# Moving the first two layernorms and the last sequence's attention and shared-expert sums inside a one-core transformer block

## The chip, the cores and the metric

The kernel runs on one core of a Trainium2 chip. The metric is the device time of one execution in microseconds (us). The unchanged kernel has a median of 1045.91 us over 3 runs (1045.9 to 1046.4). Engines are named as in the profile: PE (matrix multiply, with PEld for its weight loads), DVE (vector), ACT (activation), POOL (the engine that also issues indirect DMAs), SP (the queue that issues most plain DMAs).

## The reference, cut to what matters

The input is 16 sequences of 512 tokens of 256 numbers, float32. Each token gets its input, plus linear attention over its own sequence, plus a feed-forward part:

```python
xn = layernorm(x)
q, k, v = elu(xn@Wq+bq)+1, elu(xn@Wk+bk)+1, xn@Wv+bv          # 16 heads of 16
kv  = einsum('bkhd,bkhm->bhdm', k, v)
att = einsum('bqhd,bhdm->bqhm', q, kv) / max(q . sum(k), 1e-6) @ Wo + bo
shared = swiglu(xn @ w_in.T) @ w_out.T
# two of the four experts of the winning group, weights w_se
routed = sum_e (swiglu(xn @ w1.T) * w_se[:, e]) @ w2[e].T
out = x + att + shared + routed
```

## The kernel before, in words

The work is done in two stages. **The first stage** goes over the 16 sequences (`for b in range(B)`). For sequence b it makes keys, queries and the router's logits (`project`, L404 and L415), the routing decisions (`route`, nearly all small DVE instructions), x'k (`summarize`, `pxk`, L681), the routed experts' hidden rows (`hidden_rows`, `phr`, L587; `first_rows`, L636 for sequence 0), which go to the DRAM tensor `h_d`, and the shared expert's hidden columns (`hidden`, `phs`, L613; `first_hidden`, L655 for sequence 0), which stay in `hs_all`. `mix` (L694 to L717) turns x'k into the matrix `kvo`: four products `pvk` on PE, `vk` on DVE, two products `pm` on PE, a copy on ACT. `outputs` (L750) then sums, for each of the four tiles of 128 tokens, four products with `hs_all` and two with `qT` and `kvo` into `po`; `gather` adds that to the residual `res` (L761) and writes it to the right part of the token's row in `h_d` (L762). The projections of sequence b+1 are put in front of the rest of sequence b, and the layernorm of b+2 beside it.

**The second stage** runs over 67 tiles of 128 tokens, sorted by their pair of experts (`order` computes the sorting as a list of row numbers, in the last two sequences). Tiles are taken in pairs (`Tiles`). `rows` gathers the rows of a pair from `h_d` with one indirect DMA per tile on POOL (L902) into one of four buffers, which are the old arrays `qq_all`, `x_all`, `kk_all`, `xn_all` in turn. `turn` transposes the pair's hidden rows into `hT` (two buffers), with 12 copies on ACT (L923) and seven transposes on DVE (L929, L935). `sums` does the products with the two experts' weights on PE (`py`, L952: 8 records of 512 columns for a tile, in one of six PSUM buffers), adds the weighted products to the tile's residual part on DVE (L959, L962) and scatters the result to `out` with an indirect DMA on POOL (L965). Gathers run three pairs ahead, turns two.

**The last sequence (b = 15) is handled apart.** Its residual, without `po`, goes to `h_d` early (L999), so that it passes through the second stage like any other. Its `mix` stands inside the second stage (after the fourth pair, L1059), and its four `po` at the very end: the first before the `If` that handles surplus tiles (L1063), the other three after it. There the finished output of sequence 15 is read back from DRAM (`far`, L1081), `po` is added (L1088), and the result is written again (L1089).

**The start.** `first` does the layernorm and projections of sequence 0 in an order pinned by hand (`tc.keep_in_program_order`), tile by tile: statistics (L327, L328), root on ACT (L329), reciprocal and scaling on DVE (L330, L331), transpose on PE (L336), copy on ACT (L339), with the key and query products (L343) between the tiles. `normalize(1)` (L285 to L305) does sequence 1 without a pinned order. For later sequences `normalize` sends the result through DRAM and transposes it on DVE (L264).

What sets the order elsewhere: the program is a list of statements that a scheduler turns into one queue for each engine, by its own estimates of cost; `pin`ned statements keep their written order, `issue_after` holds a statement behind another, `high_priority` moves one up. Each engine then works its queue strictly in order.

Of the kernel before, what the change touches and what calls it, by code (L numbers as in the profile page):

```python
# [15 lines left out]
P = 128  # L16
# [5 lines left out]
def block_kernel(  # L22
# [248 lines left out]
    def normalize(b):  # L271

        xt = xs[b]
        st = small.tile([P, NT, 6], FP, tag="st", name=f"st_{b}")
        mv = small.tile([P, NT, 2], FP, tag="mv", name=f"mv_{b}")
        sd = small.tile([P, NT], FP, tag="sd", name=f"sd_{b}")
        rs = small.tile([P, NT], FP, tag="rs", name=f"rs_{b}")
        xn = xn_all[:, b % 2]

        n = 1 if b == 0 else NT  # L280
        made = []
        for g in range(0, NT, n):
            with tc.issue_after(last_xn[-1].ins) if last_xn else nullcontext():
                for t in range(g, g + n):
                    nc.vector.bn_stats(out=st[:, t, :], in_=xt[:, t, :])  # L285
            for t in range(g, g + n):
                nc.vector.bn_aggr(out=mv[:, t, :], in_=st[:, t, :])
            with tc.issue_after(last_copy[-1].ins) if last_copy else nullcontext():
                nc.scalar.activation(sd[:, g : g + n], mv[:, g : g + n, 1], AF.Sqrt, bias=eps_sb)
            nc.vector.reciprocal(rs[:, g : g + n], sd[:, g : g + n])  # L290
            for t in range(g, g + n):
                made.append(nc.vector.tensor_scalar(
                    xn[:, t, :], xt[:, t, :], mv[:, t, 0:1], rs[:, t : t + 1],
                    ALU.subtract, ALU.mult,
                ))
        last_xn[:] = made[-1:]
        xnT = work.tile([P, KD, S], FP, tag="xnT", name=f"xnT_{b}")
        if b < 2:
            for t in range(NT):
                pt = ps_mm.tile([P, KD, P], FP, tag="mm", name=f"pt_{b}_{t}")  # L300
                for c in range(KD):
                    nc.tensor.transpose(
                        pt[:, c, :], xn[:, t, :].rearrange("p (m c) -> p c m", c=KD)[:, c], ident
                    )
                last_copy.append(nc.scalar.copy(xnT[:, :, ts(t, P)], pt))  # L305
            return xn, xnT, None
        last_copy.clear()
        nc.sync.dma_start(out=xn_d[b % 2].rearrange("(t p) d -> p t d", p=P), in_=xn)
        return xn, xnT, turn(xnT, xn_d[b % 2], "xb", b, "(i c)")

    def first():

        pin = tc.keep_in_program_order
        xt, xn, kk, qq = xs[0], xn_all[:, 0], kk_all[:, 0], qq_all[:, 0]
        st = small.tile([P, NT, 6], FP, tag="st", name="st_0")
        mv = small.tile([P, NT, 2], FP, tag="mv", name="mv_0")
        sd = small.tile([P, NT], FP, tag="sd", name="sd_0")  # L320
        rs = small.tile([P, NT], FP, tag="rs", name="rs_0")
        lg = small.tile([P, NT, E + G], FP, tag="lg", name="lg_0")
        xnT = work.tile([P, KD, S], FP, tag="xnT", name="xnT_0")
        pks, pqs = [], []

        def place(t):
            pin(nc.vector.bn_stats(out=st[:, t, :], in_=xt[:, t, :]))  # L327
            pin(nc.vector.bn_aggr(out=mv[:, t, :], in_=st[:, t, :]))  # L328
            pin(nc.scalar.activation(sd[:, t : t + 1], mv[:, t, 1:2], AF.Sqrt, bias=eps_sb))  # L329
            pin(nc.vector.reciprocal(rs[:, t : t + 1], sd[:, t : t + 1]))  # L330
            last_xn[:] = [pin(nc.vector.tensor_scalar(  # L331
                xn[:, t, :], xt[:, t, :], mv[:, t, 0:1], rs[:, t : t + 1], ALU.subtract, ALU.mult
            ))]
            pt = ps_mm.tile([P, KD, P], FP, tag="mm", name=f"pt_0_{t}")
            for c in range(KD):
                pin(nc.tensor.transpose(  # L336
                    pt[:, c, :], xn[:, t, :].rearrange("p (m c) -> p c m", c=KD)[:, c], ident
                ))
            last_copy[:] = [pin(nc.scalar.copy(xnT[:, :, ts(t, P)], pt))]  # L339

        def times(to, t, w):
            for k in range(KD):
                pin(nc.tensor.matmul(  # L343
                    to, lhsT=xnT[:, k, ts(t, P)], rhs=w[:, k, :], start=(k == 0), stop=(k == KD - 1)
                ))
# [9 lines left out]

        place(0)
        place(1)
        keys(0)
        keys(1)
        queries(0)  # L360
        place(2)
        queries(1)
        keys(2)
        place(3)
        keys(3)
        queries(2)
        queries(3)
        for t in range(NT):
# [6 lines left out]
        return xn, xnT, (qq, kk, lg)  # L375

# [8 lines left out]
    def feature_map(b, y, tag):  # L385
# [8 lines left out]
        nc.vector.scalar_tensor_tensor(y, y, 0.0, low, ALU.max, ALU.add)  # L394

# [204 lines left out]

    def hidden(b, xs7):

# [21 lines left out]

        seven(f"phs_{b}", product, split, room, done, lambda n: None)
        return h, made
# [61 lines left out]

    def mix(b, xk, ksb):

        pvk = ps_mm.tile([P, KD, P], FP, tag="mm", name=f"pvk_{b}")
        for c in range(KD):
            for k in range(KD):
                nc.tensor.matmul(  # L694
                    pvk[:, c, :], lhsT=wv_sb[:, k, ts(c, P)],
                    rhs=by_quadrant(xk[:, k, :])[:, c],
                    start=(k == 0), stop=(k == KD - 1),
                )
        vk = one.tile([P, KD, P], FP, tag="vk", name=f"vk_{b}")

        with tc.high_priority():
# [8 lines left out]
            )  # L710
        pm = ps_mm.tile([P, KD, D], FP, tag="mm", name=f"pm_{b}")
        for c in range(KD):
            nc.tensor.matmul(
                pm[:, c, :], lhsT=vk[:, c, :], rhs=wo_sb[:, c, :], start=True, stop=True
            )
        kvo = one.tile([P, KD, D], FP, tag="kvo", name=f"kvo_{b}")
        nc.scalar.copy(kvo, pm)  # L717
        return kvo
# [21 lines left out]
    def outputs(b, t, qT, kvo, hs):  # L740


        if b + 2 < B or (b + 1 == B and t == 0):
            po = ps_y.tile([P, D], FP, tag="py", name=f"po_{b}_{t}")
# [4 lines left out]
        for i, (a, w) in enumerate(parts):  # L749
            step = nc.tensor.matmul(po, lhsT=a, rhs=w, start=(i == 0), stop=(i == len(parts) - 1))  # L750
            if b + 1 == B:
                tc.keep_in_program_order(step)
        return po

    def gather(b, res, qT, kvo, hs, placed, then):

        for t in range(NT):
# [4 lines left out]
            nc.sync.dma_start(out=h_d[ts(b * NT + t, P), HID:ROW], in_=res[:, t, :])  # L762
            between(b, then(t))

    def order():
# [216 lines left out]

    *normed_0, (qq, kk, lg) = first()
    normed = {0: (*normed_0, None), 1: normalize(1)}
    res = residual(0)
    feature_map(0, kk, "km")
    feature_map(0, qq, "qm")
    route(0, lg, res)
# [3 lines left out]
    for b in range(B):  # L992
# [38 lines left out]
        if b + 1 == B:  # L1031
            for w in tiles[:AHEAD]:
                w.rows()
        hs, made = hidden(b, sums7) if b else first_hidden(xnT)
        if b + 1 < B:
            kvo = mix(b, xk, ksb)
        if b + 2 == B:
            next(steps_of_order)
        if b + 1 < B:
            gather(b, res, qT, kvo, hs, normed[b + 2][2]() if b + 2 < B else None, {0: 2, 1: 2, 3: 2}.get)  # L1040
# [7 lines left out]

    for i, w in enumerate(tiles[: AHEAD - 1]):

        w.turn(made[i])
# [21 lines left out]


    first_po = outputs(B - 1, 0, qT, kvo, hs)
    rest(SURE)


    for half, queue in enumerate((nc.sync, nc.scalar)):
        far = work.tile([P, 2, D], FP, tag="hr", name=f"far_{half}", bufs=4)  # L1080
        queue.dma_start(  # L1081
            out=far, in_=out[B - 1, ts(half, 2 * P), :].rearrange("(t p) d -> p t d", p=P)
        )
        for j in range(2):
            t = 2 * half + j
            po = outputs(B - 1, t, qT, kvo, hs) if t else first_po
            y = work.tile([P, D], FP, tag="y", name=f"last_{t}", bufs=4)
            nc.vector.tensor_tensor(y, po, far[:, j], ALU.add)  # L1088
            (nc.sync, nc.scalar)[t % 2].dma_start(out=out[B - 1, ts(t, P), :], in_=y)  # L1089

# [31 lines left out]
```

## Time and profile before

| what | us |
|---|---|
| median of 3 runs | 1045.91 |
| the profiled execution | 1045.97 |
| its span in the profile | 1044.2 |
| time outside the span | 1.77 |
| PE busy | 1011.8 (97% of the span) |
| first matmul of sequence 0 starts | 5.30 |
| keys of sequence 1 start (L404) | 23.14 |
| last `phs` of sequence 15 ends | 784.11 |
| first `py` of the second stage starts | 792.48 |
| first of the last four `po` starts | 1029.41 |
| last PE work ends | 1040.63 |

How to read it: all times are from the start of the span of one profiled execution. A record in the PE rows is one pass of the array; a float32 product of 128x256 appears as two records. A wait is the idle time of an engine just before an instruction, put down to whatever released it.

### The profile page before, as it was taken

Reading aid. Unit: us, or ns where it says so; the run is one execution under the profiler, and the core shown is the slowest. Engines: PE = TensorE matmul, PEld = TensorE weight load, DVE = VectorE, ACT = ScalarE, POOL = GpSimd, SP = SyncE. Lnnn points to the kernel's source line nnn. Section 1 sums busy time; section 2 is a strip of 40 time slices with the busy share of each in tenths; the row PEclk is TensorE's granted clock in tenths of the full one; section 3 lists DMA queues with packets and bytes.
Section 4 is the critical chain, followed back from the end, with each engine's and each line's share of the span. In section 5 each row is a group of like instructions: output and inputs, shape, how many; then the busy total and the mean of one; then the engine's idle time right before and its main releaser. Section 6 shows DMA issues by size and latency. Waiting matters only on the chain. (4 is left out here: it accounts for less than half of the span.)

```text
span 1044.2 us, 12410 instructions
## 1 busy us (share of the span) xinstructions
PE 1011.8 (97%) x3704; PEld 685.2 (66%) x3704; DVE 787.8 (75%) x1976; ACT 479.1 (46%) x886; POOL 242.3 (23%) x353
## 2 busy tenths in 40 slices
PE   6999999999999999999999999999896999999998
PEld 4566868677786868686777768686672444444445
DVE  5969797978788797878786877868975666666662
ACT  2415353534344352535344443425138666667770
POOL 5202020110202021110202020211022555565541
PEclk9999999999999999999999999999998999999999
DMA  7142624425151523314141313221253445544441
GB/s 217 42 138 87 174 87 116 127 71 151 51 161 49 162 78 87 121 42 141 41 121 56 115 57 114 84 61 61 60 141 127 142 137 154 160 149 149 149 125 69
DMA packets 130436, 114.24 MB, mean 109 GB/s; under 512 B 72605, under 2 KB 114589, under 8 KB 130368
## 3 DMA queue, kind: packets, MB, share of 16 engines
q1 hardware_dynamic: 120080, 77.42, 25.3%
q0 software_dynamic: 8912, 35.21, 11.2%
q10 hardware_dynamic: 1376, 0.80, 0.3%
q8 instruction: 31, 0.51, 0.2%
q14 instruction: 37, 0.30, 0.1%
HBM read 63.52 MB, written 50.27 MB: 109 GB/s over the span
## 5 line engine op out<-in xcount | busy, mean ns | idle before, releaser
L952 PE MATMUL py<-w_sb,hT 128*128 x536 | 233.1, 598 | 8.4 <-DMA w_sb<-in_w 8.4
L952 PEld LDWEIGHTS py<-w_sb,hT 128*128 128x128 f32 x536 | 102.7, 192 | 137.7 <-issue 137.7
L750 PE MATMUL po<-wout_sb,hs_all 128*128 128x256 f32 x512 | 124.9, 382 | 1.9 <-DVE hs_all L572 1.4
L382 POOL TENSOR_TENSOR res<-x_all,bo_sb 128x256 f32<-128x256 f32 x64 | 49.0, 796 | 271.7 <-DMA h_d<-res 204.9
L750 PEld LDWEIGHTS po<-wout_sb,hs_all 128*128 128x128 f32 x512 | 95.8, 191 | 17.4 <-DVE hs_all L572 3.4
L965 POOL DMA_INDIRECT out<-y,goal x67 | 67.8, 1012 | 104.3 <-DVE y L962 95.1
L761 DVE TENSOR_TENSOR res<-po,res 128x256 f32<-128x256 f32 x60 | 25.5, 424 | 74.7 <-PE po L750 72.0
L668 POOL TENSOR_TENSOR k<-kk_all 128x512 f32<-128x512 f32 x16 | 20.9, 1309 | 261.8 <-DVE sm L450 251.9
L750 PE MATMUL po<-kvo,qT 128*128 128x256 f32 x256 | 65.9, 383 | 0.0
L587 PE MATMUL phr_w<-w_sb,ss 128*128 128x512 f32 x120 | 62.2, 600 | 3.6 <-DVE hr L566 2.2
L613 PE MATMUL phs_w<-ss,win_sb 128*128 128x256 f32 x240 | 61.6, 379 | 0.0
L613 PE MATMUL phs_t<-xnT,win_sb 128*128 128x256 f32 x240 | 61.6, 379 | 0.0
L587 PE MATMUL phr_t<-w_sb,xnT 128*128 128x512 f32 x120 | 61.3, 593 | 0.0
L404 PE MATMUL pk<-wkr_sb,xnT 128*128 128x266 f32 x240 | 58.9, 395 | 0.3 <-ACT xnT L305 0.3
L613 PE MATMUL phs_t<-ss,win_sb 128*128 128x256 f32 x240 | 59.1, 379 | 0.0
L587 PE MATMUL phr_t<-w_sb,ss 128*128 128x512 f32 x120 | 59.0, 593 | 0.0
L390 ACT ACTIVATE km<-km 128x1024 f32<-128x1024 f32 x16 | 16.9, 1058 | 90.7 <-DVE km L389 90.7
L681 PE MATMUL pxk<-kk_all,xn_all 128*128 128x256 f32 x256 | 57.9, 379 | 0.0
L923 ACT COPY hb<-qq_all 32x256 f32<-32x256 f32 x108 | 43.4, 402 | 26.2 <-DMA qq_all<-h_d,source 22.8
L415 PE MATMUL pq<-w_sb,xnT 128*128 128x256 f32 x240 | 54.2, 379 | 0.0
L750 PEld LDWEIGHTS po<-kvo,qT 128*128 128x128 f32 x256 | 47.5, 190 | 8.9 <-ACT kvo L717 3.0
L681 PEld LDWEIGHTS pxk<-kk_all,xn_all 128*128 128x128 f32 x256 | 48.6, 190 | 6.6
(215 smaller groups left out, 1936.3 us busy)
## 6 DMA issues: line engine op xcount, KB each, us to landing
h_d<-hr SPq DMA_DIRECT2D x64, 256.0 KB, 2.4
q_d<-qq_all SPq DMA_DIRECT2D x16, 512.0 KB, 2.8
qb<-q_d SPq DMA_DIRECT2D x64, 128.0 KB, 3.0
w_sb<-in_w SPq DMA_DIRECT2D x64, 128.0 KB, 3.5
h_d<-res SPq DMA_DIRECT2D x60, 129.0 KB, 1.9
x_all<-in_x SPq DMA_DIRECT2D x15, 512.0 KB, 5.3
xn_d<-xn_all SPq DMA_DIRECT2D x14, 512.0 KB, 3.5
xb<-xn_d SPq DMA_DIRECT2D x56, 128.0 KB, 3.0
```

The costliest lines, as they stand in the source:

```text
L382: nc.gpsimd.tensor_tensor(res[:, t, 0:D], xt[:, t, :], bo_sb, ALU.add)
L404: nc.tensor.matmul(pk, lhsT=xnT[:, k, ts(t, P)], rhs=wkr_sb[:, k, :], start=(k == 0), stop=(k == KD - 1),)
L415: nc.tensor.matmul(pq[:, t, :], lhsT=xnT[:, k, ts(t2 + t, P)], rhs=wq_sb[:, k, :], start=(k == 0), stop=(k == KD - 1),)
L587: tc.keep_in_program_order(nc.tensor.matmul(to, lhsT=xs7[i][:, ts(u, P)], rhs=w1_in[W7[i]], start=start, stop=stop, skip_group_check=True,))
L613: tc.keep_in_program_order(nc.tensor.matmul(split(to)[:, f, :], lhsT=win_in[W7[i]][:, ts(2 * u + f, P)], rhs=xs7[i], start=start and f == ...
L668: nc.gpsimd.tensor_tensor(k2, kk[:, 0:2, :], kk[:, 2:4, :], ALU.add)
L681: nc.tensor.matmul(pxk[:, c, :], lhsT=xn[:, t, ts(c, P)], rhs=kk[:, t, :], start=(t == 0), stop=(t == NT - 1),)
L750: step = nc.tensor.matmul(po, lhsT=a, rhs=w, start=(i == 0), stop=(i == len(parts) - 1))
L761: nc.vector.tensor_tensor(res[:, t, 0:D], po, res[:, t, 0:D], ALU.add)
L923: nc.scalar.copy(there[ts(q, Q), a - near, 0:n, :], self.hg[ts(a, Q), 0:n, ts(q, W)])
L952: nc.tensor.matmul(py.rearrange("p j d -> p (j d)"), lhsT=self.hT[:, f, ts(j, P)], rhs=w2_sb[:, f, bass.ds(regs[i % TR], 2 * D)], start=(f ...
L965: stored = nc.gpsimd.indirect_dma_start(out=out_rows, out_offset=bass.IndirectOffsetOnAxis(ap=self.goal[:, i : i + 1], axis=0), in_=y, in_ ...
```

## The change

Three things are done.

1. **The start.** The layernorm of sequence 1 is moved into `first`, and both are pinned: all four tiles of sequence 0 are measured and scaled, with the transposes one tile behind; then the keys, then the queries; then the bias additions, the statistics of sequence 1 between them; then its scaling and its transposes. The residual of sequence 0 is told to follow the query feature map.
2. **The last sequence.** `mix` is split in `values` (`pvk`, `vk`) and `mix` (`pm`, `kvo`). For sequence 15 both are put inside `hidden`, after the third and the ninth of its fourteen products, in PSUM buffers of the other pool (`py`). After `hidden`, the first two turns are written, and `gather_last` does all 48 records of `po` in two PSUM buffers (first all products with `kvo`, then all with `hs_all`), adds them to `res` and writes it to `h_d` in two DMAs of 256 tokens. The block at the end of the kernel (read back, add, write again) is gone.
3. **The second gather.** The first three pairs are still gathered early, for their hidden rows. Pairs 0 and 1 are gathered again in front of the loop, and pair 2 inside its first round behind the gathers of pair 3, so that their residual part is the finished one.

```diff
     def first():
+        for t in range(NT):
+            measure(0, t)
+            scale(0, t, 1)
+            if t:
+                place(0, t - 1)
+        keys(0)
+        place(0, NT - 1)
+        for t in range(1, NT):
+            keys(t)
+        for t in range(NT):
+            queries(t)
+        for t in range(2):
+            keep(t)
+        for t in range(NT):
+            measure(1, t)
+        for t in range(2, NT):
+            keep(t)
+        scale(1, 0, NT)
+        for t in range(NT):
+            place(1, t)
...
+    with tc.issue_after(feature_map(0, qq, "qm").ins):
+        res = residual(0)
...
+    def gather_last(b, res, qT, kvo, hs):
+        pos = [ps_y.tile([P, 2, D], FP, tag="py", name=f"po_{b}_{i}") for i in range(NT // 2)]
...
+        for t in range(NT):
+            add([(qT[:, c, ts(t, P)], kvo[:, c, :]) for c in range(KD)], t, True, False)
+        for t in range(NT):
+            add([(hs[:, f, ts(t, P)], wout_sb[:, f, :]) for f in range(KH)], t, False, True)
+        for i, po in enumerate(pos):
+            to = res[:, 2 * i : 2 * i + 2, 0:D]
+            with tc.high_priority():
+                nc.vector.tensor_tensor(to, po, to, ALU.add)
+            nc.sync.dma_start(
+                out=h_d[ts(b * NT // 2 + i, 2 * P), HID:ROW].rearrange("(t p) h -> p t h", p=P),
+                in_=res[:, 2 * i : 2 * i + 2, :],
+            )
...
+            def then(n):
+                if n == 2:
+                    made_of["vk"] = values(b, xk, ksb)
+                if n == 8:
+                    made_of["kvo"] = mix(b, made_of["vk"])
...
+        if b + 1 == B:
+            for i, w in enumerate(tiles[: AHEAD - 1]):
+                w.turn(made[i])
+            gather_last(b, res, qT, kvo, hs)
...
+    for w in tiles[: AHEAD - 1]:
+        w.rows()
     for g, w in enumerate(tiles):
         if g + AHEAD < len(tiles):
             tiles[g + AHEAD].rows()
         if g + AHEAD - 1 < len(tiles):
             tiles[g + AHEAD - 1].turn()
+        if g == 0:
+            tiles[AHEAD - 1].rows()
         w.sums()
-        if g == AHEAD:
-            kvo = mix(B - 1, xk, ksb)
...
-    first_po = outputs(B - 1, 0, qT, kvo, hs)
     rest(SURE)
-    for half, queue in enumerate((nc.sync, nc.scalar)):
-        far = work.tile([P, 2, D], FP, tag="hr", name=f"far_{half}", bufs=4)
...
-            po = outputs(B - 1, t, qT, kvo, hs) if t else first_po
-            y = work.tile([P, D], FP, tag="y", name=f"last_{t}", bufs=4)
-            nc.vector.tensor_tensor(y, po, far[:, j], ALU.add)
-            (nc.sync, nc.scalar)[t % 2].dma_start(out=out[B - 1, ts(t, P), :], in_=y)
```

More of the change, by code (lines that the diff above doesn't have):

```diff
@@ L278, in normalize @@
         xn = xn_all[:, b % 2]
-        n = 1 if b == 0 else NT
         made = []
-        for g in range(0, NT, n):
+        for g, n in [(0, NT)]:
             with tc.issue_after(last_xn[-1].ins) if last_xn else nullcontext():
@@ L297, in normalize @@
         xnT = work.tile([P, KD, S], FP, tag="xnT", name=f"xnT_{b}")
[L298 to L306, printed above, removed]
         last_copy.clear()
@@ L316, in first @@
         pin = tc.keep_in_program_order
[L317 to L321, printed above, removed]
+        stats = []
+        for b in range(2):
+            stats.append([
+                small.tile([P, NT, n], FP, tag=tag, name=f"{tag}_{b}")
+                for tag, n in (("st", 6), ("mv", 2), ("sd", 1), ("rs", 1))
+            ])
@@ L322, in first, with measure @@
+        kk, qq = kk_all[:, 0], qq_all[:, 0]
         lg = small.tile([P, NT, E + G], FP, tag="lg", name="lg_0")
-        xnT = work.tile([P, KD, S], FP, tag="xnT", name="xnT_0")
+        xnT = [work.tile([P, KD, S], FP, tag="xnT", name=f"xnT_{b}") for b in range(2)]
         pks, pqs = [], []
-        def place(t):
-            pin(nc.vector.bn_stats(out=st[:, t, :], in_=xt[:, t, :]))
+        def measure(b, t):
+            st, mv, _, _ = stats[b]
+            pin(nc.vector.bn_stats(out=st[:, t, :], in_=xs[b][:, t, :]))
@@ L328, in place, with scale @@
             pin(nc.vector.bn_aggr(out=mv[:, t, :], in_=st[:, t, :]))
[L329 to L334, printed above, removed]
+        def scale(b, t, n):
+            _, mv, sd, rs = stats[b]
+            pin(nc.scalar.activation(sd[:, t : t + n, 0], mv[:, t : t + n, 1], AF.Sqrt, bias=eps_sb))
+            pin(nc.vector.reciprocal(rs[:, t : t + n], sd[:, t : t + n]))
+            for i in range(t, t + n):
+                last_xn[:] = [pin(nc.vector.tensor_scalar(
+                    xn_all[:, b, i, :], xs[b][:, i, :], mv[:, i, 0:1], rs[:, i], ALU.subtract, ALU.mult
+                ))]
@@ L335, in place @@
+        def place(b, t):
+            pt = ps_mm.tile([P, KD, P], FP, tag="mm", name=f"pt_{b}_{t}")
             for c in range(KD):
                 pin(nc.tensor.transpose(
-                    pt[:, c, :], xn[:, t, :].rearrange("p (m c) -> p c m", c=KD)[:, c], ident
+                    pt[:, c, :], xn_all[:, b, t, :].rearrange("p (m c) -> p c m", c=KD)[:, c], ident
                 ))
-            last_copy[:] = [pin(nc.scalar.copy(xnT[:, :, ts(t, P)], pt))]
+            last_copy[:] = [pin(nc.scalar.copy(xnT[b][:, :, ts(t, P)], pt))]
@@ L343, in times @@
                 pin(nc.tensor.matmul(
-                    to, lhsT=xnT[:, k, ts(t, P)], rhs=w[:, k, :], start=(k == 0), stop=(k == KD - 1)
+                    to, lhsT=xnT[0][:, k, ts(t, P)], rhs=w[:, k, :], start=(k == 0), stop=(k == KD - 1)
                 ))
@@ L354, in queries, with keep @@
             times(pqs[-1][:, t % 2, :], t, wq_sb)
[L356 to L368, printed above, removed]
+        def keep(t):
             pin(nc.vector.tensor_tensor(kk[:, t, :], pks[t][:, 0:D], bkr_sb[:, 0:D], ALU.add))
             pin(nc.vector.tensor_tensor(lg[:, t, :], pks[t][:, D:KR], bkr_sb[:, D:KR], ALU.add))
+        for t in range(NT):
[18 more added lines that the diff above has]
+            place(1, t)
         for i, pq in enumerate(pqs):
@@ L374, in first @@
             )
-        return xn, xnT, (qq, kk, lg)
+        return xnT, (qq, kk, lg)
     def residual(b):
@@ L393, in feature_map @@
             nc.scalar.activation(low, low, AF.Exp, scale=-1.0)
-        nc.vector.scalar_tensor_tensor(y, y, 0.0, low, ALU.max, ALU.add)
+        return nc.vector.scalar_tensor_tensor(y, y, 0.0, low, ALU.max, ALU.add)
     def project(b, xnT):
@@ L599, in hidden_rows, with hidden @@
         seven(f"phr_{b}", product, lambda a: a, room, done, lambda n: between(b, then(n)))
-    def hidden(b, xs7):
+    def hidden(b, xs7, then=lambda n: None):
         h = hs_all
@@ L623, in done @@
                 made.append((silu, product))
-        seven(f"phs_{b}", product, split, room, done, lambda n: None)
+        seven(f"phs_{b}", product, split, room, done, then)
         return h, made
@@ L687, in summarize, with small_sums, values @@
         return xk
-    def mix(b, xk, ksb):
-        pvk = ps_mm.tile([P, KD, P], FP, tag="mm", name=f"pvk_{b}")
+    def small_sums(b, shape, name):
+        if b + 1 == B:
+            return ps_y.tile(shape, FP, tag="py", name=f"{name}_{b}"), tc.keep_in_program_order
+        return ps_mm.tile(shape, FP, tag="mm", name=f"{name}_{b}"), lambda step: step
+    def values(b, xk, ksb):
+        pvk, pin = small_sums(b, [P, KD, P], "pvk")
         for c in range(KD):
             for k in range(KD):
-                nc.tensor.matmul(
+                pin(nc.tensor.matmul(
                     pvk[:, c, :], lhsT=wv_sb[:, k, ts(c, P)],
@@ L697, in mix @@
                     start=(k == 0), stop=(k == KD - 1),
-                )
+                ))
         vk = one.tile([P, KD, P], FP, tag="vk", name=f"vk_{b}")
@@ L710, in mix @@
             )
-        pm = ps_mm.tile([P, KD, D], FP, tag="mm", name=f"pm_{b}")
+        return vk
+    def mix(b, vk):
+        pm, pin = small_sums(b, [P, KD, D], "pm")
         for c in range(KD):
-            nc.tensor.matmul(
+            pin(nc.tensor.matmul(
                 pm[:, c, :], lhsT=vk[:, c, :], rhs=wo_sb[:, c, :], start=True, stop=True
-            )
+            ))
         kvo = one.tile([P, KD, D], FP, tag="kvo", name=f"kvo_{b}")
-        nc.scalar.copy(kvo, pm)
+        with tc.high_priority() if b + 1 == B else nullcontext():
+            nc.scalar.copy(kvo, pm)
         return kvo
@@ L740, in outputs @@
     def outputs(b, t, qT, kvo, hs):
-        if b + 2 < B or (b + 1 == B and t == 0):
+        if b + 2 != B:
             po = ps_y.tile([P, D], FP, tag="py", name=f"po_{b}_{t}")
@@ L749, in outputs @@
         for i, (a, w) in enumerate(parts):
-            step = nc.tensor.matmul(po, lhsT=a, rhs=w, start=(i == 0), stop=(i == len(parts) - 1))
-            if b + 1 == B:
-                tc.keep_in_program_order(step)
+            nc.tensor.matmul(po, lhsT=a, rhs=w, start=(i == 0), stop=(i == len(parts) - 1))
         return po
@@ L763, in gather, with add @@
             between(b, then(t))
+    def gather_last(b, res, qT, kvo, hs):
+        pos = [ps_y.tile([P, 2, D], FP, tag="py", name=f"po_{b}_{i}") for i in range(NT // 2)]
+        def add(parts, t, begin, end):
+            for i, (a, w) in enumerate(parts):
+                tc.keep_in_program_order(nc.tensor.matmul(
+                    pos[t // 2][:, t % 2, :], lhsT=a, rhs=w, start=begin and i == 0 and t % 2 == 0,
+                    stop=end and i == len(parts) - 1, skip_group_check=True,
+                ))
+        for t in range(NT):
[10 more added lines that the diff above has]
+            )
     def order():
@@ L981, in block_kernel @@
     waiting = list(range(G * NL))
-    *normed_0, (qq, kk, lg) = first()
-    normed = {0: (*normed_0, None), 1: normalize(1)}
-    res = residual(0)
+    first_xnT, (qq, kk, lg) = first()
+    normed = {b: (xn_all[:, b], first_xnT[b], None) for b in range(2)}
     feature_map(0, kk, "km")
-    feature_map(0, qq, "qm")
+    with tc.issue_after(feature_map(0, qq, "qm").ins):
+        res = residual(0)
     route(0, lg, res)
@@ L1033, in block_kernel @@
                 w.rows()
-        hs, made = hidden(b, sums7) if b else first_hidden(xnT)
         if b + 1 < B:
-            kvo = mix(b, xk, ksb)
+            hs, made = hidden(b, sums7) if b else first_hidden(xnT)
+            kvo = mix(b, values(b, xk, ksb))
+        else:
+            def then(n):
[3 more added lines that the diff above has]
+                    made_of["kvo"] = mix(b, made_of["vk"])
+            made_of = {}
+            hs, made = hidden(b, sums7, then)
+            kvo = made_of["kvo"]
         if b + 2 == B:
             next(steps_of_order)
-        if b + 1 < B:
+        if b + 1 == B:
+            for i, w in enumerate(tiles[: AHEAD - 1]):
+                w.turn(made[i])
+            gather_last(b, res, qT, kvo, hs)
+        else:
             gather(b, res, qT, kvo, hs, normed[b + 2][2]() if b + 2 < B else None, {0: 2, 1: 2, 3: 2}.get)
@@ L1047, in block_kernel @@
     )
-    for i, w in enumerate(tiles[: AHEAD - 1]):
-        w.turn(made[i])
+    for w in tiles[: AHEAD - 1]:
+        w.rows()
     for g, w in enumerate(tiles):
@@ L1072, in rest @@
                 rest(i + STEP)
-    first_po = outputs(B - 1, 0, qT, kvo, hs)
     rest(SURE)
-    for half, queue in enumerate((nc.sync, nc.scalar)):
-        far = work.tile([P, 2, D], FP, tag="hr", name=f"far_{half}", bufs=4)
[L1081 to L1085, printed above, removed]
-            po = outputs(B - 1, t, qT, kvo, hs) if t else first_po
-            y = work.tile([P, D], FP, tag="y", name=f"last_{t}", bufs=4)
-            nc.vector.tensor_tensor(y, po, far[:, j], ALU.add)
-            (nc.sync, nc.scalar)[t % 2].dma_start(out=out[B - 1, ts(t, P), :], in_=y)
 def kernel(**inputs):
```

## The prediction

> **What bounds the kernel now.** I read the busy shares first, then what the tensor engine waits for, then the chain that ended last, and only then the three places that the change touches. Lines of the page:
>
> ```profile
> PE 1011.8 (97%) x3704; PEld 685.2 (66%) x3704; DVE 787.8 (75%) x1976; ACT 479.1 (46%) x886; POOL 242.3 (23%) x353
> ...
> PE 1%; DVE 0%; issue 0%
> ```
>
> PE is busy 97% of the span, so 1044.2 - 1011.8 = 32.4 us is all that can be won without taking work from PE. The chain holds only the last 1%: before it PE simply works on. So the question is where those 32 us lie. The waits of PE (line waited for, by whom: us in total, times, longest):
>
> ```profile
> PE py L952 <- DMA w_sb<-in_w: 8.4, 1, 8.4
> PE pt L336 <- DVE xn_all L331: 7.0, 2, 5.3
> PE pm L713 <- DVE rz L729: 2.5, 1, 2.5
> PE phr_w L587 <- DVE hr L566: 2.2, 7, 0.3
> PE pt L302 <- DVE xn_all L292: 2.2, 1, 2.2
> PE pm L713 <- DVE vk L708: 2.2, 1, 2.2
> ```
>
> Row 1 is the step from the first to the second stage, rows 2 and 5 are the start, row 6 is the late `mix` of the last sequence. Row 4 is nearly all that PE waits between 80 and 730 us, so the sequences in the middle run at PE's pace. The windows show that an idle PE costs twice (window, length, busy PE, PEld, DVE, ACT, POOL, granted clock, DMA share, GB/s):
>
> ```profile
> 23.00:27.00 4.00, 3.85 (x10) 3.04 (x11) 2.48 (x8) 1.30 (x6) 0.20 (x1) 0.57 0.27 97
> ...
> 784.00:792.00 8.00, 0.10 (x1) 0.00 (x0) 6.46 (x15) 7.59 (x18) 0.25 (x1) 0.73 0.89 299
> 792.00:796.00 4.00, 3.52 (x4) 1.50 (x5) 1.58 (x4) 3.85 (x11) 0.00 (x0) 0.50 0.01 4
> 824.00:828.00 4.00, 2.09 (x7) 1.44 (x8) 3.54 (x10) 2.50 (x7) 1.04 (x2) 1.00 0.56 182
> ```
>
> PE stands still from 784.11 to 792.48, and then runs at a clock of .50. After the shorter idle of row 5, at 21.4, it ran at .57; after row 6's 2.2 us, at 826, it kept 1.00.
>
> **Change 1, the start: -3.0.** Before, the root of tile 3 stands on ACT behind the copy of tile 2, which waited for PE:
>
> ```profile
> 13.52 0.37 ACT L339 COPY xnT<-pt 128x256 f32<-128x256 f32 x1 [4.58 <-PE pt L336]
> ...
> 21.40 1.45 PE L302 MATMUL pt<-ident,xn_all 128*128 128x128 f32 x8 [2.22 <-DVE xn_all L292]
> 23.14 5.47 PE L404 MATMUL pk<-wkr_sb,xnT 128*128 128x266 f32 x16 [0.30 <-ACT xnT L305]
> ```
>
> After, no root waits for PE: the first three tiles took 2.4 us each from statistics to scaling (statistics at 5.07, 7.50 and 9.55), so tile 3 is scaled at about 9.9 instead of 15.2. PE then does the first keys to 10.9 (still slow: .47 us a record), the other twelve key records and tile 3's transposes to 14.9, 16 query records of .215 to 18.3. DVE has, behind the keys of 0 and 1 (13.7), the statistics of sequence 1 (2.4, to 16.2), the other bias additions (to 17.3), `qq` (.7) and the four scalings (1.4): 19.6. The transposes end at 20.1, and sequence 1's keys, 16 x .223 = 3.6 us at full clock in place of 5.47, at 23.7 instead of 28.5: a lead of 4.7.
>
> The lead isn't all kept, since DVE becomes late. x_2's load is issued at 19.90 behind the weights, and its statistics waited for it until 24.52; nothing moves that load. The residual told to follow the feature map keeps its place in POOL's order, so this instruction of the diff costs nothing; what hides it is POOL, 23% busy. `pxk` of sequence 0 needs the key feature map, about 27.5: lead 4.4. Then DVE works without a gap to 64 us; of its work only some 1.2 us has been done earlier, and each `phs` L655 (50.49, .37 waited for `hr` L643) needs a buffer that DVE frees: lead 3.1 there. At `pm` L713 (66.95, freed by `vk` L708 at 66.86) it is 2.8 to 3.0, with one `qT` transpose of 1.24 now queued behind `vk`. I take -3.0; the ends are -4.7 (all kept) and 0 (DVE bound by x_2's load all the way). From there PE bounds, and the lead stays. DVE's order in the middle is shuffled by small statements; bounds ±3.3, what PE waits there in all; I take 0.
>
> **Change 2a, between the stages: -2.1.** Before, from the end of `phs` (784.11) to the end of `py` (1029.41), 245.3 us: 8.37 idle, 2.9 lost to the clock (5.4 us at half pace), 67 tiles x 3.43 = 229.7, `pvk` and `pm` 1.7, their wait 2.17, and .46 of small gaps. After: `pvk` and `pm` (1.7) stand inside `hidden`, between products, six of the fourteen products apart, so that PE has other work while DVE makes `vk`; 48 records of `po` x .2145 = 10.3 fill the idle, in which the weights of the second stage land anyway (they let `py` go at 792.48, and `po` ends at 796); so neither the 8.4 nor the 2.9 nor the 2.17 return. 1.7 + 10.3 + 229.7 + .46 + 1.0 (change 3) = 243.2 against 245.3: -2.1, bounds with those of change 3. The `po` work itself, 10.3, is only moved: it is taken off in the tail's sum.
>
> If the cover fails, that is if `po` had to wait for `res` or `kvo`, the price would be the idle again, up to 2.9 of clock besides. Here `kvo` is due five products ahead, and the products with `hs_all` stand last in `po`; so I count none. The skill has a rule on this: the Trainium skill, "TensorE: Matmul & The Clock Gate", Part 1, says that the clock falls only after an idle window of about 3.4 us and needs about 3.4 us of work to come back. The trace differs from it: 2.2 us of idle at 21.4 sufficed for .57, and after 8.4 us the half pace lasted 5.4. By the page the clock's price would be an estimated 1.7 in place of 2.9, and the time 1.2 later than mine.
>
> **Change 3, the second gathers: +1.0 of stalls (counted above), 0 to +5.8.** They are six more indirect DMAs on POOL. One is issued in about 1.0 (the 67 scatters L965: 1012 ns) and landed 3.7 to 3.9 after its issue (8.7 at most, beside weight loads). They wait for both `res` writes: the last `po` (796 on the clock of before), the addition on DVE in the order between the two thirds of `hT_2` (798.3), the write of 264 KB (2.4, as `h_d<-hr`): 800.8. Then POOL issues pairs 0 and 1 (801.0 to 805.8), pair 3's two, and the first scatters; queued behind these stand the outputs, and six PSUM buffers let PE run 6 tiles, 20.6 us, ahead of DVE's `y`. `y_0` starts at 804.9, pair 3's rows land at 811.2, its 12 copies on ACT (5.0) end at 816.6, and PE wants them at 816.5; pair 4's at 824.3 against 823.5. From there a pair costs POOL 5.1 (two gathers and two scatters of 1.0, .27 apart), ACT 5.0 and PE 6.86, so the loop recovers. Hence about 1 us. If the gathers take 8.7 instead of 3.9, +4.8 more. The skill speaks against such gathers: "DMA: Bandwidth & Descriptors", the section on SWDGE, HWDGE and iDMA, says that DVE's two-port modes lock GpSimd out where it writes descriptors. The trace doesn't show it (67 gathers of 946 to 1053 ns with DVE 40 to 76% busy).
>
> **Change 2b, the tail: -9.1.** Before:
>
> ```profile
> 1029.41 1.89 PE L750 MATMUL po<-wout_sb,hs_all 128*128 128x256 f32 x8
> ...
> 1030.89 0.98 POOL L965 DMA_INDIRECT out<-y,goal  x1 [2.46 <-DVE y L962]
> ...
> 1035.17 0.40 SPq L1081 DMA_DIRECT2D far<-out  x1
> ...
> 1038.25 1.09 DVE L1088 TENSOR_TENSOR last<-po,far 128x256 f32<-128x256 f32 x3 [7.63 <-DMA far<-out]
> ```
>
> From `py`'s end at 1029.41 to 1044.2 are 14.8 us. After, the last tile's two DVE steps (.2 + .99), .28, the scatter (.98) and its landing remain: `far` on SP was let go 4.28 after that scatter began, which takes in issue and landing. 1.2 + .28 + 4.28 = 5.7, bounds ±.7. 5.7 - 14.8 = -9.1.
>
> **Sum.** -3.0 - 2.1 - 9.1 = -14.2: span 1030.0, and with the 1.77 outside it (1045.97 - 1044.2) 1031.8. The profiled execution stands .06 above the median, so nothing is corrected.
>
> **Rivals.** (1) All of the front's 4.7 is kept and the ring never stalls: 1031.8 - 1.7 - 1.0 = 1029.1. For it: PE bounds from 80 us on; against: DVE's unbroken row to 64 us. (2) The front gives nothing, since DVE waits for x_2 at 24.52 as before and sets `phs` and `pm`: 1034.8. For it: the unmoved load. Against: DVE's own work is less by 1.2 and `pxk` comes earlier. (3) The second gathers starve PE, landing in 8.7 beside the w2 and residual traffic: 1031.8 + 4.8 = 1036.6. For it: the stretch 784 to 792 moved 299 GB/s. Against: the same gathers later took 3.9. (4) Slower: the loop starts with fewer tiles in hand, and POOL's queue, with gather behind scatter behind `y`, never recovers. It decides from a pair's period of 7.29 on (6.86 + 14.2/33); at 7.4, +.54 for each of 33 pairs, it is 17.8 more, 1049.6. Against it POOL's 5.1 a pair. In what is queued on POOL a late gather holds up the scatters behind it, and these free `y`. (5) No change: the gains are given back in part by this loop, with a period of 7.28 a pair 14 us, so 1045.9. That the change doesn't do what it says is real only for the residual's place, priced at nothing above.
>
> **Chances.** Forecast .50, (1) .10, (2) .18, (3) .15, (4) .05, (5) .02. Within 0.2% (2.1 us) is about what a measurement of this kernel can tell from no change; so faster .93, same .02, slower .05. The range takes (1) to (3) with the ±.7 of the tail: 1028.5 to 1037.0.
>
> **What would show it.** Right: keys of sequence 1 end near 23.7 and without half pace, `phs` L655 starts near 47, `po` of the last sequence follows `hidden` without idle, `py` starts about 10.3 us after the end of `phs` at full clock, the last `py` ends at about 1024.3, and 5.7 us follow. Wrong: PE rows waiting for `hT` or `y` at 805 to 830, a wait of `po` for `res`' buffer or `hs_all`, idle at `phs` L655 as large as the lead. The sum falls if x_2's load or the gather's landing differ from the rows used.

## The result, and the profile after

The changed kernel takes 1034.36 us (median of 4, 1033.23 to 1034.62) against 1046.16 (1045.9 to 1048.25): a ratio of 0.9881, 95% interval 0.9864 to 0.9898. I had forecast 1031.8, range 1028.5 to 1037.0. The profiled execution took 1033.23; its span is 1031.5, so 1.7 lies outside.

The page of the changed kernel, first its busy row, then its chain that ended last:

```profile
PE 1004.9 (97%) x3704; PEld 681.7 (66%) x3704; DVE 779.4 (76%) x1974; ACT 488.1 (47%) x893; POOL 254.8 (25%) x359
...
POOL 0%; POOLq 0%
```

The chain now ends on POOL, no longer on PE and DVE. PE's waits (line waited for, by whom: total, times, longest):

```profile
PE pt L335 <- DVE xn_all L328: 7.5, 5, 5.3
PE pm L731 <- DVE rz L748: 2.5, 1, 2.5
PE phr_w L595 <- DVE ss L538: 1.9, 1, 1.9
PE py L993 <- DVE hT L976: 1.6, 1, 1.6
PE phs L663 <- DVE hr L651: 1.5, 1, 1.5
PE po L768 <- DVE hs_all L580: 1.4, 5, 0.3
PE phr_w L595 <- DVE hr L574: 0.3, 1, 0.3
```

The 8.4 for the weights is gone, and so are the waits of 2.2 in front of `pt` (start) and `pm` (last sequence). New are 1.6 for `hT` and 1.5 in the first sequence (0.4 before). What I hadn't forecast is the last row: `phr_w` waited seven times for `hr` (2.2 in all), now once.

The seam of the two stages, first in PE's timeline (start, busy time, what):

```profile
779.48 3.62 PE L788 MATMUL po<-kvo,qT 128*128 128x256 f32 x16
782.93 7.07 PE L788 MATMUL po<-wout_sb,hs_all 128*128 128x256 f32 x32
789.84 20.76 PE L993 MATMUL py<-w_sb,hT 128*128 x48
```

The same seam in windows (length, busy PE, PEld, DVE, ACT, POOL, granted clock, DMA share, GB/s):

```profile
784.00:792.00 8.00, 8.00 (x34) 6.09 (x33) 5.26 (x12) 7.73 (x20) 0.00 (x0) 1.00 0.10 33
792.00:796.00 4.00, 4.00 (x11) 1.85 (x10) 0.00 (x0) 3.46 (x9) 0.87 (x1) 1.00 0.18 66
```

`po` fills the idle without a gap, and the clock stays at 1.00 where it was .50.

Where the 12.74 us between the spans (1044.25 and 1031.51) lie, by the lead of the same PE statement over the kernel before:

| stretch | lead at its end | gained | forecast |
|---|---|---|---|
| start, to sequence 1 (first `pxk`) | 2.64 | 2.64 | 3.0 |
| sequences 2 to 13 | 5.72 | 3.08 | 0 |
| sequence 14 (no half clock behind its wait) | 6.22 | 0.50 | 0 |
| to the end of the last `py` (1029.58, now 1022.20) | 7.38 | 1.16 | 2.1 |
| tail (14.67, now 9.31) | 12.74 | 5.36 | 9.1 |

Two rows had to be explained: a gain of 3.1 that nobody ordered, and a tail that is 3.7 short. The 0.50 of sequence 14 is the balance of two things: before, PE lost about 1.5 to half clock behind the wait for `rz` (736.85 to 739.83 at .50), and now it waits 1.9 for `ss` instead of 1.3.

### The profile page after: what moved, and what is told of

The parts are those of the page before. It is cut to its first block, busy times and chain, and to the rows that moved or that the text cites. A ratio compares the mean times of both kernels' runs of the same rounds, so it can differ in the third digit from the quotient of the medians.

```text
span 1031.5 us, 12407 instructions
## 1 busy us (share of the span) xinstructions
PE 1004.9 (97%) x3704; PEld 681.7 (66%) x3704; DVE 779.4 (76%) x1974; ACT 488.1 (47%) x893; POOL 254.8 (25%) x359
## 5 line engine op out<-in xcount | busy, mean ns | idle before, releaser
L993 PE MATMUL py<-w_sb,hT 128*128 x536 | 230.7, 592 | 1.7 <-DVE hT L976 1.6
L768 PE MATMUL po<-wout_sb,hs_all 128*128 128x256 f32 x480 | 116.6, 380 | 1.4 <-DVE hs_all L580 1.4
L768 PEld LDWEIGHTS po<-wout_sb,hs_all 128*128 128x128 f32 x480 | 89.2, 190 | 15.1 <-DVE hs_all L580 3.4
L768 PE MATMUL po<-kvo,qT 128*128 128x256 f32 x240 | 61.7, 383 | 0.0
L412 PEld LDWEIGHTS pk<-wkr_sb,xnT 128*128 128x128 f32 x240 | 45.4, 190 | 8.0
```

Of the source, the lines that this page charges most:

```text
L412: nc.tensor.matmul(pk, lhsT=xnT[:, k, ts(t, P)], rhs=wkr_sb[:, k, :], start=(k == 0), stop=(k == KD - 1),)
L993: nc.tensor.matmul(py.rearrange("p j d -> p (j d)"), lhsT=self.hT[:, f, ts(j, P)], rhs=w2_sb[:, f, bass.ds(regs[i % TR], 2 * D)], start=(f ...
```

## The experiments

**The middle.** In the kernel before, DVE scales `xn` of the next sequence while POOL makes the residual. Its timeline at 134 to 138 us:

```profile
134.73 0.82 DVE L292 TENSOR_SCALAR xn_all<-x_all,mv,rs 128x256 f32<-128x256 f32 x1
135.37 2.88 POOL L382 TENSOR_TENSOR res<-x_all,bo_sb 128x256 f32<-128x256 f32 x4
135.47 0.70 DVE L469 TENSOR_TENSOR beats<-pe 128x24 f32<-128x24 f32 x1
136.10 0.87 DVE L292 TENSOR_SCALAR xn_all<-x_all,mv,rs 128x256 f32<-128x256 f32 x1
136.89 0.71 DVE L470 TENSOR_TENSOR wins<-wins,beats 128x24 f32<-128x24 f32 x1
...
138.32 0.17 DVE L471 TENSOR_TENSOR wins<-wins,beats 128x24 f32<-128x24 f32 x1
```

A `wins` step takes .71 beside POOL's additions and .17 once they are over; a scaling .87, where it takes .40 alone. In the changed kernel the additions come later, behind the routing's counting. The group of the scalings, in the kernel before and in the changed one (count: shortest, median, longest in ns, first and last start):

```profile
L292 DVE TENSOR_SCALAR xn_all<-x_all,mv,rs x60: 392/820/1244, 20.9 to 662.4; 128x256 f32<-128x256 f32 x60
L290 DVE TENSOR_SCALAR xn_all<-x_all,mv,rs x56: 320/402/1242, 47.6 to 656.7; 128x256 f32<-128x256 f32 x56
```

Between 125 and 385 us all 24 scalings are long before (the first two of each four beside POOL's `k`, the others beside the residual) and none is in the changed kernel. The Trainium skill, "SBUF — State Buffer", section "Who interferes with whom", states a rule for this: DVE and GpSimd share a pair of ports as an exclusive lock, and of two instructions that need it, whichever comes second stands still until the other is done. That it is the ports no run here shows, but the rows agree: DVE starts one step for each of POOL's additions (135.47 to 137.52, .68 apart on average; POOL's four take 2.88, .72 each).

Theory A: this order on POOL is the 3.1. Theory B: the earlier start leaves DVE early enough, whatever POOL does.

*e1, the start alone* (the hunks of `first`, `normalize` and the residual, nothing else).

> Only the start is changed (part 1); the last sequence and the second stage are those of before. Theory A: the start is worth 2.6 us by itself, and the 3.1 us that the trace of after gains between 140 and 390 us (six waits of phr_w for DVE's hr, gone) come from the place of the residual's additions in POOL's order, which is here the one of before. So 1046.0 - 2.6 = 1043.4, and the six waits of about .32 are there again. Rival B: those waits went because the start leaves DVE earlier; then 1046.0 - 5.7 = 1040.3 and no such wait.

Measured: 1040.19 against 1045.74 (ratio 0.9951, 0.9934 to 0.9968), 5.55 less. No wait of `phr_w` on `hr` in the middle; lead 3.1 at sequence 1, 6.2 from sequence 8 on.

*e3, the changed kernel with a free residual.*

```diff
-    with tc.issue_after(feature_map(0, qq, "qm").ins):
-        res = residual(0)
+    res = residual(0)
+    feature_map(0, qq, "qm")
```

> The changed kernel without the one statement that the residual of sequence 0 follows the query feature map: the residual is written between the two feature maps instead. Its POOL order in sequences 3 to 8 is the one of before (additions ahead of the routing's small ones). Theory A: 3.1 us slower than after, 1034.4 + 3.1 = 1037.5, with the six waits of phr_w of .32 back. Rival B (the waits went with the earlier start): 1034.4, no waits.

Measured: 1033.67 (ratio 0.9886, 0.9869 to 0.9902). The times are those of B, but the premise was wrong: both traces show the new order on POOL (`k`, `wins`, `ahead_of`, `res`) in sequences 3 to 8, not that of before. The scheduler makes that order from the changed start alone. So e1 and e3 don't decide between A and B, and e2, with the old start and the old order, can't either; e4 and e5 do.

*e2, parts 2 and 3 alone.*

> Only parts 2 and 3 (the last sequence's sums in front of the second stage, the second gathers); the start is that of before. Theory A: 1.2 between the stages and 5.3 at the tail, nothing in the middle, since POOL's order in sequences 3 to 8 is the one of before: 1046.0 - 6.5 = 1039.5, up to 1.1 more or less by whether a short wait of PE costs a piece of half clock. The tail from the last py to the span's end is 9.3, not 5.7, with a DRAIN of about 3.4 on POOL in it. Rival B: the tail costs what I predicted, 5.7, and the 9.3 belonged to this one profile: 1036.

Measured: 1039.30 (ratio 0.9944, 0.9927 to 0.9961), tail 9.31: A. Its 6.4 and the 5.55 of e1 add up to 12.0, where the whole change gained 11.8. POOL's order is the old one, and among PE's waits are those of before:

```profile
PE phr_w L587 <- DVE hr L566: 2.2, 7, 0.3
...
PE py L985 <- DVE hT L968: 1.6, 2, 0.8
```

*e4, the kernel before with the residual's additions behind the counting ones, from sequence 1 on.*

```diff
+        with tc.issue_after(route(b, lg, res).ins):   # route returns its last POOL addition
+            fill(b, res)                              # the four additions of residual
```

> The kernel before, with one thing: in every sequence from 1 on the residual's additions on POOL stand behind the routing's counting additions, so that they no longer run beside DVE's scaling of xn. No part of the change is in it. Theory A: POOL's additions and DVE's scalings slow each other (402 ns alone, 961 beside POOL, in before), that makes hr late; so 1046.0 - 3.1 = 1042.9 or a little below, as the later sequences gain too. Rival C: POOL's order is only a symptom, DVE's own order makes the difference: 1046.0, the waits stay.

Measured: 1042.39 (ratio 0.9967, 0.9956 to 0.9978), 3.35 less with no part of the change in it. In its timeline at the same place the steps behind `k` are short (of the 24 scalings between 125 and 385 us, the 12 beside the residual are .40 again, the 12 beside `k` stay long):

```profile
135.34 0.40 DVE L292 TENSOR_SCALAR xn_all<-x_all,mv,rs 128x256 f32<-128x256 f32 x1
135.66 0.17 DVE L475 TENSOR_TENSOR wins<-wins,beats 128x24 f32<-128x24 f32 x1
```

*e5, the changed kernel with POOL's old order* (in sequences 3 to 9 the counting additions and the next `wins` are held behind the residual; DVE's and PE's order stays).

> The changed kernel with one thing put back: in sequences 3 to 9 the residual's additions stand in POOL's queue ahead of the routing's small POOL statements, as in before (DVE's and PE's own order are those of after). The first runs left this open: the start alone, and the change with a free residual, both got the new POOL order, so they couldn't tell the two apart. Theory A (POOL's additions beside DVE's scalings make hr late): the scalings take .87 instead of .40 again, phr_w waits .3 in about six sequences, 1034.4 + 3.1 = 1037.5. Rival B (DVE is early enough by the new start, whatever POOL does): 1034.4 and no waits.

Measured: 1045.19 (ratio to the kernel before 0.9987, 0.9977 to 0.9996). The six waits are back, .58 each, and the lead falls from 1.8 at sequence 1 to -.2 at sequence 8, where in the changed kernel it grows from 2.6 to 5.7. One of the six in PE's timeline:

```profile
142.07 1.13 PE L599 MATMUL phr_w<-w_sb,ss 128*128 128x512 f32 x2 [0.58 <-DVE hr L578]
```

So A holds: POOL's order alone is worth 3.4 in the old kernel, and putting it back costs 5.1 in the new one up to sequence 8 (3.1 gained there, 2.0 lost here). DVE's own order as the cause (C) falls with it: in e4 as in e5 the order on PE, DVE and ACT in the first 700 us is that of the kernel it was made from, and POOL's alone differs. The 5.1 is more than I expected, as each wait is .58 and not .32. From one `pxk` to the next, sequences 3 to 8 take 47.9 before, 47.4 in the changed kernel, 47.35 in e4 and 48.3 in e5. So a wait of .32 costs about .50 and one of .58 about .84, mostly because records of PE overlap (.43 from start to start at .59 each) and behind a wait that overlap is missing. The other half of e5's loss lies in the second stage: a second wait of `py` for `hT`, 4.8. I come back to it.

**The tail.** At the program's end POOL's queue has an instruction that the profile calls `DRAIN`. From the view of that line in the kernel before (read like the scalings):

```profile
L1118 POOLq DRAIN  x3: 51/103/2928, 1035.0 to 1044.0; - x3
```

And from the same view of the changed kernel:

```profile
L1161 POOLq DRAIN  x3: 51/103/3418, 1027.2 to 1031.2; - x3
```

Before, the long one ran from 1035.0 to 1037.9 beside the last `po`. Now nothing is beside it: scatter 1023.52, landed 1025.81, the closing semaphore statement of the `If` on POOL (1.0, to 1027.2), `DRAIN` to 1030.6, .9 more.

*e7, six idle additions on POOL behind the last scatter.*

```diff
     rest(SURE)
+    old = x_all.rearrange("p a b c -> p (a b c)")[:, 0:512]
+    for _ in range(6):
+        nc.gpsimd.tensor_tensor(old, old, old, ALU.add)
```

> The changed kernel with six idle additions of 128x512 on POOL behind the last scatter (6 x 1.31 = 7.9 us; their result is used by nobody). It asks what the 3.4 us DRAIN on POOL at the end waits for. Theory A: for the last scatter, so that it ends 7.0 to 7.1 after that scatter's start, whatever POOL does meanwhile (1030.89 to 1037.89 in before, 1023.52 to 1030.61 in after): the DRAIN shrinks to nearly nothing, and the tail from the last py grows from 9.3 to about 12 (additions to 1032.4, 1.0 and .9 behind them). Rival B: it is a fixed price of the program's end: 3.4 once more behind the additions, tail 15.5.

Measured: tail 16.1, as B has it; the additions took 6.6, and the `DRAIN` ended 3.44 after the last of them (1040.38 to 1043.83). *e8, without the `If`* (the `rest(SURE)` line removed).

> The changed kernel without the If for surplus tiles at its end (for these inputs no surplus tile is filled, so the output stays the same). Theory A: the DRAIN belongs to the last scatter, tail 9.3 as before. Rival B: the DRAIN and the 1.0 us semaphore statement ahead of it are the price of the If's block on POOL: tail 5 to 6, which is what I predicted.

Measured: tail 6.56; the `DRAIN` ended 3.43 after the scatter's end. The same line in e7 and in e8 (here it starts before POOL's last statement is through, so it is longer):

```profile
L1164 POOLq DRAIN  x3: 51/109/4517, 1039.3 to 1044.4; - x3
L1160 POOLq DRAIN  x3: 46/109/4638, 1031.3 to 1036.5; - x3
```

In e8 neither theory holds as it stands: the tail falls, against A, but the `DRAIN` stays, against B; that 6.56 comes near B's 5 to 6 is chance. With the changed kernel itself, e7 and e8 show that the `DRAIN` ends about 3.4 behind POOL's last statement, be it an addition, a scatter or the closing of the `If`, and that the `If` adds 2.75 by waiting for the landing and its own 1.0. What the `DRAIN` does in that time no run here shows. By their times (1046.45 and 1038.47, one execution each) these two say nothing, as both have the second `py` wait of 4.5.

**The second gathers.** *e10, without them.*

> The changed kernel without the six second gathers: the first three pairs keep the rows that they gathered early, so the tokens of the last sequence in them lack the attention and shared-expert sums (this part of the result is left out). Theory A: the second gathers cost the wait of 1.6 and nothing else: 1034.4 - 1.6 = 1032.8, no py wait. Rival B: they cost more than the wait shows, in clock or in outputs that come late: below 1031.

Measured: 1031.91 (ratio 0.9867, 0.9842 to 0.9892), no `py` wait. Beside it *e9, the changed kernel again*:

> The changed kernel itself, unchanged, beside the next two. Three kernels with its second stage (residual early, POOL work behind, no If) had a second wait of py for hT_8, of 4.5 to 4.8, that its own first profile hasn't. Theory A: that wait goes with those programs or their timing, and the changed kernel keeps 1034.4 with one wait of 1.6. Rival B: it depends on the chip or the moment, and the changed kernel has it here too: about 1039.

Measured: 1034.03, with two waits of 1.0 and 1.1: A. So the second gathers cost 2.1, which is those two waits. That is A in e10 too, with a larger price than its 1.6: counted from one `py` record's start to the next, waits cost PE 2.2 in the first profile of the changed kernel, 2.6 in e9 and nothing in e10. Two ways to place them otherwise:

```diff
-    for w in tiles[: AHEAD - 1]:
+    for w in [tiles[AHEAD], *tiles[: AHEAD - 1]]:        # e6
+    for w in (tiles[0], tiles[AHEAD], tiles[1]):         # e11
         w.rows()
     for g, w in enumerate(tiles):
-        if g + AHEAD < len(tiles):
+        if g and g + AHEAD < len(tiles):
```

> The changed kernel with pair 3's first gathers in front of the second gathers of pairs 0 and 1, not behind them. Theory A: the wait of py for hT (1.59 in after at 812) is the queue on POOL and nothing else; it goes, as y_0 may be late (PE has six buffers, 20.6 us): 1034.4 - 1.6 = 1032.8. Rival B: the outputs come 2.5 later, PE waits for a buffer instead: 1034.4 or more.

Measured: 1035.47 (ratio 0.9894, 0.9878 to 0.9911). The wait for `hT_6` (the transposed rows of the pair that starts with tile 6) goes, but one of 2.86 for `hT_4` comes at 806. That is B's time, but not its buffer: the transposes of `hT_4` stand in DVE's queue behind `y_0`, which waits for its second gather until 802.5.

> The changed kernel with pair 3's first gathers between the second gathers of pair 0 and pair 1. In front of both they made py wait 2.9 for hT_4, since y_0 and y_1 then held up the transposes of hT_4 in DVE's queue. Theory A: here y_0 and y_1 come as in after and pair 3's rows land 2.5 earlier, so neither wait is left: 1032.8. Rival B: y_2, which needs pair 1, stands ahead of hT_6's transposes in DVE's queue and holds them up as much: 1034.4 or more.

Measured: 1034.08 (ratio 0.9890, 0.9863 to 0.9916). The wait at 812 goes, one of 1.92 at 820 takes its place, for `hT_8`, whose rows now land late (DVE waits 2.5 for them, to 814.8), which neither theory had. Neither of the two orders won anything; that the late `res` has to be paid somewhere in these pairs is my reading, not shown.

**The longest wait left.** *e12, `pvk` and `pm` of sequence 14 inside `hidden` too.*

> The changed kernel, with the small products of the last but one sequence (pvk, pm) put inside its hidden products too, in the same places as the change does for the last. Its pm waits 2.47 for DVE (the normalizer rz stands ahead of vk in DVE's queue) at 731 in after, the longest wait of PE that is left behind the start. Theory A: vk comes early in DVE's queue, the wait goes, and with it the piece of half clock that followed it in some executions: 1034.1 - 2.5 = 1031.6, down to 1030.5. Rival B: the wait only moves, to the products with qT or with hs_all, which come behind the same rz chain on DVE: 1034.1.

Measured: 1034.60 (ratio 0.9888, 0.9871 to 0.9904). B: the 2.5 before `pm` go, `po` waits 1.0 for `hs_all` and `phr_w` 3.0 for `ss` instead of 1.9, as PE's waits in e12 say:

```profile
PE phr_w L595 <- DVE ss L538: 3.0, 1, 3.0
PE po L770 <- DVE hs_all L580: 2.4, 6, 1.0
```

There DVE is the bound (in the changed kernel it is busy without a gap from 728 to 736), and a different order on PE doesn't help. No version that computes the whole for all inputs beat the changed kernel clear of the noise (e3's 1033.67 is within it).

**What stays open.** e5, e7 and e8 have a second wait of `py` (4.5 to 4.8) for `hT_8`: DVE's first transposition of it stood about 7 us, though its rows had landed, until 821 (826 in e5). It needs a buffer that PE frees, and PE's own semaphore updates are recorded only then (in e7 those of the products that ended at 811.3, 816.2 and 819.7 all stand at 821.0 to 821.3). The changed kernel has no such wait in either profile, and e3, e6, e11 and e12, with the same or a like order, haven't either. I found no cause.

## Why the prediction was right, and where not

The sum was 2.6 too low (1.5 by the spans; the profiled execution of the changed kernel is 1.1 below its median). That it is in range is partly luck: two errors offset each other, and without the 3.1 of the middle the time would be 1037.4, just outside.

- **Start, -3.0: right.** 2.64 in the profile (2.8 in e9, 3.1 in e1). Sequence 1's keys end at 24.07 (forecast 23.7) at full clock, the whole lead of 4.4 is there at `pxk`, and DVE takes 1.5 of it back at `phs`, as forecast, though not at its first record (45.99, forecast 47) but at the ninth (51.22, behind `hr`). The lateness of the keys is POOL beside DVE once more: the four scalings of sequence 1, taken at 1.4, took 2.8 (2.2 in e1 and e9), since they now run beside the residual of sequence 0 (POOL, 13.90 to 19.55). Rival 2 (nothing kept) falls by its mechanism, though its number, 1034.8, is the nearest of all.
- **The middle, 0 with a bound of 3.3: mis-sized.** I took DVE's reshuffled order as neutral and looked at what PE waits for, not at why `hr` is late. The step that failed is "I take 0"; the mechanism is POOL beside DVE, 3.1. Its rows stood in the trace of before: scalings from 392 to 1244 ns in one group. And the row of `hr` isn't "nearly all" that PE waited between 80 and 730 us, but 1.9 of 3.3; the other 1.4 are five waits of `po` for `hs_all`, which stayed.
- **Between the stages, -2.1: right in kind.** No idle, no half clock, no `pm` wait. It gave 1.2; the term that was too small is the ring of the second gathers, 2.2 to 2.6 from start to start instead of 1.0, at the place named (812 instead of 816), within its bounds. The first of these gathers landed in 3.9, as taken, but the ones queued behind it in 4.5 to 5.1, pair 3's last rows among them; rival 3 (8.7) didn't come.
- **Tail, -9.1 with a bound of .7: wrong size.** "The scatter and its landing remain" left out the `DRAIN` (3.42) and the .9 behind it. The 4.28 for the scatter was misread too: the scatter landed 2.94 after its start, and the other 1.34, until `far` was let go, took in the `If`'s closing statement on POOL (1034.0 to 1034.9); so that statement was in the sum under another name. Now the landing takes 2.29, which gives .65 back. Before, closing statement and `DRAIN` lay beside the last `po` (1034.0 to 1037.9), so they were in the trace, with cover; the change takes that cover away. 9.31 instead of 5.7.
- **The residual of sequence 0** kept its place (13.90; 13.63 before), and the statement costs nothing: e3 has the same time within its interval.
- **Rivals 1, 4 and 5** (all kept and no stall, slower, same) fall: 1.5 of the lead is taken back, the ring does stall, and the loop recovers after two pairs. By mechanism the forecast's own case is the nearest, with the middle and the tail off.

## What to carry to other kernels

When the last work of a kernel is taken away, read what the other engines do in that time, their closing statements too: they become the tail. When a small step varies by a factor of two or more in one group, look what runs on POOL beside it, before trusting an order that the scheduler made. A wait that is cured on an engine in order comes back as the next statement's, if the engine behind it is the bound.

## What the runs showed of the hardware

- POOL's `DRAIN` at the end costs 3.4 behind POOL's last statement (3.42 to 3.44 in the changed kernel, e7 and e8; 2.93 in the kernel before, for which no run shows the reason), and .9 more follow.
- A DVE step with POOL's addition beside it takes .70 to .87 instead of .17 to .40.
- Half clock comes in pieces of 3.41 us or multiples (before: 3.41 from 23.0 and from 736.4, 10.24 from 787.6; these starts lie 209 and 15 steps of 3.413 apart). The same wait of 2.5 in front of `pm` was followed by such a piece in e9 (from 730.7, with the wait from 728.4 to 730.9) and not in the first profile of the changed kernel, where a step of the grid parts the wait (729.6, counted back 87 steps from the fall of the clock at 1026.6; wait from 728.7 to 731.1). In sequence 14 the first profile gained .50 on the kernel before, e9 lost .11. The Trainium skill, "TensorE: Matmul & The Clock Gate", Part 1, speaks of a window of 3413 ns that runs freely; the grid agrees. That a whole window must be idle doesn't: in e3 1.9 us within one step sufficed (wait from 745.3 to 747.2, half clock from 747.3).
